# A sorted edge's record in DRAM: 64 bytes at multiples of 64 in place of 24 bytes side by side, in a four-layer graph network kernel

## The chip, the cores and the metric

The kernel runs on one core of one Trainium2 chip. The time is the device time of one execution, in microseconds. Nine executions of the kernel before took 2677.39 to 2699.86 us, with a median of 2693.03 us.

The names of the engines in the profile: PE is TensorE's matrix multiplication and PEld its weight load, DVE is VectorE, ACT is ScalarE, POOL is GpSimd, SP is SyncE, and SPq is SP's queue of DMAs. Transfers issued by SP run one after another on that queue, shared out over 16 DMA engines.

## The reference

The kernel computes four residual graph layers over 3125 nodes with 96 features and 100000 edges that are sorted by destination. Each layer takes the row-wise normalised and rectified features and adds its result to `x`.

```python
h = jnp.maximum(_layernorm(x, axis=-1), 0.0)
x = x + _L0_gnn_ref(h, edge_index)       # 10 hops: out = spmm(out) * 0.9 + h * 0.1
h = jnp.maximum(_layernorm(x, axis=-1), 0.0)
x = x + _L1_gnn_ref(h, src, dst, W, b)   # softmax over each node's incoming edges
h = jnp.maximum(_layernorm(x, axis=-1), 0.0)
x = x + _L2_gnn_ref(h, edge_index, edge_attr, ...)
h = jnp.maximum(_layernorm(x, axis=-1), 0.0)
x = x + _L3_gnn_ref(h, edge_index, ...)  # two graph convolutions
```

What matters for this case is layer 2, the only one that needs data per edge. For every edge it forms a message from the features of both ends and from four edge attributes, and sums the messages of each destination:

```python
node_feat = _mlp(x, W_node, b_node, g_node, beta_node)
edge_feat = _mlp(edge_attr, W_edge, b_edge, g_edge, beta_edge)
row, col = (edge_index[0], edge_index[1])
message = jnp.concatenate([x[row], x[col], edge_feat], axis=1)
message = _mlp(message, W_msg, b_msg, g_msg, beta_msg)
agg = jax.ops.segment_sum(message, col, num_segments=N)
return agg + node_feat
```

`_mlp` is a matrix product, a rectification and a normalisation over all rows (with the mean and the variance over all edges, for the messages).

## The kernel before, in words

All the work is in `narrow` (a second version, `wide`, runs only when a flag says that a bound did not hold; here it doesn't run). Its stages follow one another: a prelude that builds count tables from the edge list, layer 0 with its ten hops, layer 1, layer 2, layer 3. Nodes are kept in `NB` = 25 blocks of 128. A hop is a product of a table of edge counts (`A8`, 25 by 25 blocks of 128 x 128, 8-bit floats) with the features: for each block of nodes 25 weight loads and 25 matmuls (`gather`, L409). What follows a pair of blocks is in `onward`: VectorE scales and adds (L635, L637) and splits the sum into a high and a low half for the next hop.

**Sorting edges.** Layer 2 wants 48128 of the edges grouped by their source, in bins of 125 nodes. These edges are dealt with in three groups `GA` of 125, 125 and 126 columns of 128 edges. `in_bins(g, ...)` works out each edge's place `addr` on VectorE in many small steps and then sends each edge's record to that place. A record is 12 numbers of 16 bits, 24 bytes: the four attributes as high parts, their four low parts, a one, two small numbers that say where the edge's two ends lie, and one unused. The records of 14 columns are put together on POOL in one of two tiles `rec2` (L550 to L553), and then POOL issues one indirect DMA for each column (L555): 128 records, one from each partition, to the rows of `recs[g]` in DRAM that `addr` names. A place is partition-major: `addr` is the partition times `CG` = 152, plus 25 times the bin, plus a rank. So `recs[g]` has 128 x 152 = 19456 places, more than there are edges. The places that no edge takes must hold a harmless record; the prelude fills all places with it from the tile `blank` (L346 to L351), with one store for each group on SP's queue.

The steps of `in_bins` are a generator that `beside` advances twice in each pair of blocks from the second hop on. So the sort runs beside layer 0's hops: VectorE, TensorE and ScalarE work at the hops and at a first pass over the edge attributes (`eps`, L666 to L669, fed by SP's loads L664), and POOL issues the scatters.

**Reading the records back.** At the start of layer 1, `in_fields(g)` (L785) loads a group's records as 128 rows of 152 records (L788, SP's queue, two buffers `recs2`). VectorE takes the eleventh number of each into `rlA`, in six slices (L791) and copies that into `rf` (L797); ScalarE copies the first ten numbers into `rf`, reordered (L796). Then, four places at a time, TensorE turns a piece of `rf` (L803), ScalarE copies it from PSUM (`fts`, L805), and SP stores it to `fields` in DRAM (L807), from where layer 2 reads it. These are generators as well: layer 1's loop over its 25 blocks advances group 0 from block 2 on, group 1 from block 7 and group 2 from block 16. A scheduler decides the final order of the instructions on each engine: it has moved the parts of `in_fields` that need only the load ahead of the loop's order, to layer 1's beginning.

Layer 1's block is 50 matmuls with their weight loads into one of two PSUM buffers `hop` (L816); then `lo` (ScalarE, L819), `both` (VectorE, L821), `den` and `z` (VectorE), a transpose `zp` (L831) that ScalarE copies into `zT` (L833), a product `op` (L835) that is added to `x` (VectorE, L836); then the normalisation of the new rows, whose `hb` is on ScalarE (L394), and two tables `Pt` and `Qt` of layer 2, stored by SP (L853). Each engine goes through its instructions in order, so an instruction that waits holds up those behind it on that engine.

Layer 2 (from 1741 us) fetches rows of 384 bytes from `Pt` by the sources of the edges, with 408 indirect DMAs on POOL (L1024), from DRAM into SBUF; no records are written there.

Of the kernel before, what the change touches and what calls it, by code (L numbers as in the profile page):

```python
# [11 lines left out]
F16 = mybir.dt.float16  # L12
# [9 lines left out]
P = 128  # L22
# [22 lines left out]
GA = [(0, 125), (16000, 125), (32000, 126)]  # L45
BINS, BN = 25, 125
SL, CAP = 6, 768
CG = 152
UA = len(GA) * CG // 4
AHEAD = 1440  # L50
# [16 lines left out]
def narrow(ctx: ExitStack, tc: tile.TileContext, a: dict, out: bass.AP, flag: bass.AP):  # L67


    nc = tc.nc  # L70
    V, S, G, T = nc.vector, nc.scalar, nc.gpsimd, nc.tensor

    const = ctx.enter_context(tc.tile_pool(name="const", bufs=1))
    dram = ctx.enter_context(tc.tile_pool(name="dram", bufs=1, space=DRAM))
# [2 lines left out]
    Pt = dram.tile([NP, 2 * D], F16, name="Pt")  # L77
    Qt = dram.tile([NP + 2 * P, 2 * D], F16, name="Qt")
    Sd = [dram.tile([NP + 2 * P, D], F32, name=f"Sd{i}") for i in range(2)]
    recs = [dram.tile([P * CG, 12], F16, name=f"recs{i}") for i in range(len(GA))]  # L80

    fields = dram.tile([UA, 44, P], F16, name="fields")
    rlT_d = dram.tile([P, Q * 8], F16, name="rlT_d")
# [73 lines left out]
    with tc.tile_pool(name="edges", bufs=1) as sp, tc.tile_pool(name="onehot", bufs=3) as hp, tc.tile_pool(name="handed", bufs=2) as hd, \  # L157
# [119 lines left out]
        for n, g in enumerate(order):  # L277
# [13 lines left out]
            for s in ((0, 1) if n == 0 else (upward,)):  # L291
                line = up if s else down
                at = line.index(g) + 1 if s == upward else 0
                if at < len(line):
                    handed[s] = hd.tile([P, NB], F16, name=f"handed{s}")
                    c = column_of(line[at]) + (0 if s else WIN - 1)
# [45 lines left out]
        for t in Sd:  # L342
            nc.sync.dma_start(t.rearrange("(b p) d -> p b d", p=P), zero[:, None, :D].to_broadcast([P, NB + 2, D]))
        nc.sync.dma_start(Qt[NP:].rearrange("(b p) d -> p b d", p=P),
                          zero.bitcast(F16)[:, None, :2 * D].to_broadcast([P, 2, 2 * D]))
        blank = sp.tile([P, CG, 12], F16, name="blank")  # L346
        G.memset(blank, 0.0)
        G.memset(blank[:, :, 9:10], 200.0)
        G.memset(blank[:, :, 10:11], 4000.0)
        for t in recs:  # L350
            nc.sync.dma_start(t.rearrange("(p c) k -> p (c k)", p=P), blank.rearrange("p c k -> p (c k)"))  # L351


        src = a["edge_attr_T"].rearrange("k (s c) -> (k s) c", s=25)
# [84 lines left out]
    r, m = norm(0, NB)  # L439
# [24 lines left out]
    def in_bins(g, rp, ep):  # L464
# [4 lines left out]
        si, di, b, t, w, mv = (room[:, 1040 + 126 * i:1040 + 126 * i + C] for i in range(6))  # L469
# [60 lines left out]
        p, lo, hi = mv.bitcast(I32), scan.bitcast(I32), t.bitcast(I32)  # L530
# [14 lines left out]
        ea = a["edge_attr_4"][e0:e0 + n].rearrange("(p c) k -> p c k", p=P)  # L545
        for c0 in range(0, C, 14):
            n = min(14, C - c0)
            r = rec2[(c0 // 14) % 2]
            et = rp.tile([P, 14, 4], F32, name="ea2", bufs=2)[:, :n, :]
            G.dma_start(et, ea[:, c0:c0 + n])  # L550
            G.tensor_copy(r[:, :n, 0:4], et)
            G.tensor_tensor(r[:, :n, 4:8], et, r[:, :n, 0:4], ALU.subtract)
            G.tensor_copy(r[:, :n, 9:11], lane2[:, c0:c0 + n, :])  # L553
            for c in range(n):
                ins = G.indirect_dma_start(  # L555
                    out=recs[g], out_offset=bass.IndirectOffsetOnAxis(ap=addr[:, c0 + c:c0 + c + 1], axis=0),
                    in_=r[:, c, :], in_offset=None, bounds_check=P * CG - 1, oob_is_err=False)
                if c0 + c:
                    tc.declare_no_dep(ins.ins, group=f"recs{g}", reason="each edge has a row of its own")
                tc.add_to_no_dep_group(f"recs{g}", ins.ins)  # L560
            yield

    with tc.tile_pool(name="l0", bufs=1) as lp, tc.tile_pool(name="l0p", bufs=3, space=PSUM) as pp:
        A8 = lp.tile([P, NB, NP], F8, name="A8")
        dc = lp.tile([P, NB], F32, name="dc")
        u = up.tile([P, NB, 2 * D + 2], F16, name="u")
        V.memset(u[:, :, 2 * D:], 1.0)
        with tc.tile_pool(name="l0t", bufs=4, space=PSUM) as tp:
            V.memset(none.bitcast(I32), 0)
            for k in range(NB):  # L570
# [12 lines left out]
                if k % 5 == 4:  # L583
                    g = slice(k - 4, k + 1)
                    V.tensor_reduce(cnt_dst[:, g], sums[:, g, :], AX.X, ALU.add)
                    t = small.tile([P, 5], F32, name="deg")
# [16 lines left out]
        em = None  # L603
        tri16 = room[:, 2304:2368].bitcast(F16)
        V.tensor_scalar(tri16, lane, part, None, ALU.is_gt)
        rec2 = [lp.tile([P, 14, 12], F16, name=f"rec2{i}") for i in range(2)]
        for t in rec2:
            G.memset(t, 0.0)
            G.memset(t[:, :, 8:9], 1.0)
        with tc.tile_pool(name="l0e", bufs=3, space=PSUM) as ep, tc.tile_pool(name="l0r", bufs=1) as rp, \  # L610
                tc.tile_pool(name="l0o", bufs=1, space=PSUM) as op:
            binning = itertools.chain(*(in_bins(g, rp, op) for g in range(len(GA))))
            for step in range(K_HOPS):
                last = step == K_HOPS - 1
                whole = up.tile([P, NB, 2 * D + 2], F16, name="u")
# [79 lines left out]
                spare, u = u, new  # L695
# [69 lines left out]
    with tc.tile_pool(name="l1", bufs=1) as lp, tc.tile_pool(name="l1w", bufs=3) as wp, \  # L765
# [19 lines left out]
        def in_fields(g):  # L785

            r = lp.tile([P, CG, 12], F16, name="recs2", bufs=2)
            nc.sync.dma_start(r.rearrange("p c k -> p (c k)"), recs[g].rearrange("(p c) k -> p (c k)", p=P))  # L788
            for i in range(SL):
                c = slice(i * BINS, (i + 1) * BINS if i < SL - 1 else CG)  # L790
                V.tensor_scalar(rlA[:, g * CG + c.start:g * CG + c.stop], r[:, c, 10], relB[:, g * SL + i:g * SL + i + 1], None,  # L791
                                ALU.subtract)
            rf_ = lp.tile([P, CG * 11 + P - 44], F16, name="rf", bufs=2)
            V.memset(rf_[:, CG * 11:], 0.0)
            rf = rf_[:, :CG * 11].rearrange("p (u f j) -> p u f j", f=11, j=4)
            S.activation(rf[:, :, :10, :], r.rearrange("p (u j) f -> p u f j", j=4)[:, :, :10, :], AF.Copy)  # L796
            V.tensor_copy(rf[:, :, 10, :], rlA[:, g * CG:(g + 1) * CG].rearrange("p (u j) -> p u j", j=4))  # L797
            yield
            for u0 in range(0, CG // 4, 4):
                n = min(4, CG // 4 - u0)  # L800
                ps = qp.tile([P, 4, P], F32, name="ft")[:, :n, :]
                for i in range(n):
                    T.matmul(ps[:, i, :], rf_[:, 44 * (u0 + i):44 * (u0 + i) + P], ident16, start=True, stop=True)  # L803
                t = wp.tile([44, 4, P], F16, name="fts")[:, :n, :]
                S.activation(t, ps[:44], AF.Copy)  # L805
                at = g * CG // 4 + u0
                nc.sync.dma_start(fields[at:at + n].rearrange("u f e -> f u e"), t)  # L807
                yield
# [3 lines left out]
        for b in range(NB):  # L812
# [7 lines left out]
            t = wp.tile([P, 2, D], F32, name="both")  # L820
# [17 lines left out]
            r, m = norm(b, 1)  # L838
# [343 lines left out]
    with tc.tile_pool(name="l3", bufs=1) as lp, tc.tile_pool(name="l3w", bufs=3) as wp, \  # L1182
# [78 lines left out]
        for b0 in range(0, NB, 5):  # L1261
            g = slice(b0, b0 + 5)
# [597 lines left out]
```

## Time and profile before

The profile is of one execution that took 2685.9 us; the span from its first to its last instruction is 2683.6 us. Busy time by stage, in us (the windows' bounds are read from the timeline, and rounded):

| window, us | stage | PE | DVE | ACT | POOL | TensorE clock | DMA share |
|---|---|---|---|---|---|---|---|
| 0 to 104 | prelude, first part | 16.27 | 57.10 | 8.08 | 33.35 | 0.93 | 0.27 |
| 104 to 480 | prelude, count tables | 277.92 | 324.27 | 281.25 | 12.30 | 0.93 | 0.04 |
| 480 to 1565 | layer 0, sort of edges | 653.38 | 436.80 | 278.14 | 398.59 | 0.76 | 0.04 |
| 1565 to 1741 | layer 1 | 150.55 | 129.54 | 73.25 | 2.27 | 0.94 | 0.16 |
| 1741 to 2510 | layer 2 | 604.85 | 439.32 | 232.36 | 420.11 | 0.92 | 0.41 |
| 2510 to 2683 | layer 3 | 139.45 | 94.63 | 46.74 | 5.97 | 0.88 | 0.10 |
| whole span | | 1842.4 | 1481.7 | 919.8 | 872.6 | | |

A share over the whole span is a mean over stages with different limits; the table is read a stage at a time. The clock is the share of its full rate that TensorE was granted. The scatters of L555 run from 586.7 to 1254 us, in three bursts, one for each group.

How the profile's lines are read. A group's line has the line of the program, the engine, the operation, out<-in with the tiles' names, the shapes, how often it came, then its busy time in us and the mean of one in ns, and after the second bar the time that the engine stood idle just before these instructions and what ended most of that. A line of the timeline has the start and the duration in us, then engine, line and operation, the count where several were joined, and in brackets the idle time ahead of it with what ended it. "issue" is time in which the engine waited for nothing that the profile shows; "remote" is a wait that the profile puts down to no instruction of this core. A line of windows has the stretch and its length in us, then for PE, PEld, DVE, ACT and POOL the busy time with the count, the clock, the share of the DMA engines and GB/s.

### The profile page before, as it was taken

What the parts mean: (1) busy time and instruction counts of PE and PEld (TensorE: products, weight loads), DVE (VectorE), ACT (ScalarE), POOL (GpSimd) and SP (SyncE); (2) the same over time, 40 slices, a digit from 0 to 9 for tenths busy, and PEclk for the clock granted to TensorE, in tenths of its full rate; (3) what the DMA queues carried; (4) which work ended last, traced back from release to release, by engine and by line L of the source; (5) the groups of instructions that cost most, each with busy time, mean ns of one, the idle gap of its engine ahead of it and who ended that gap; (6) DMA issues with size and microseconds to landing.
All of it is one profiled execution on the core that took longest, in us unless ns stands there. A gap on an engine that the chain in (4) does not pass through costs nothing. (4 is left out here: it accounts for less than half of the span.)

```text
span 2683.6 us, 51385 instructions
## 1 busy us (share of the span) xinstructions
PE 1842.4 (69%) x19447; PEld 1477.7 (55%) x19447; DVE 1481.7 (55%) x4400; ACT 919.8 (34%) x2334; POOL 872.6 (33%) x928
## 2 busy tenths in 40 slices
PE   0477777881366128313999988858888787788698
PEld 0223335760155007202999978646666666677588
DVE  3778999880046006201664587736665555555853
ACT  0488847370166003000331253313333332222340
POOL 4100000017723771675000000065555555554000
PEclk9789999985578558655999999979999999989799
DMA  4100000000000000000000011134444444334200
GB/s 119 57 9 1 1 1 3 8 10 4 4 9 9 4 4 10 5 4 5 10 10 19 2 47 30 32 97 101 107 107 109 106 101 107 89 96 100 55 1 20
DMA packets 133737, 108.21 MB, mean 40 GB/s; under 512 B 93607, under 2 KB 103341, under 8 KB 133479
## 3 DMA queue, kind: packets, MB, share of 16 engines
q1 hardware_dynamic: 106117, 79.60, 11.3%
q0 software_dynamic: 25952, 22.03, 4.5%
q8 instruction: 154, 2.52, 0.4%
q10 hardware_dynamic: 1410, 3.20, 0.4%
q14 instruction: 104, 0.85, 0.1%
HBM read 86.43 MB, written 18.29 MB: 39 GB/s over the span
## 5 line engine op out<-in xcount | busy, mean ns | idle before, releaser
L409 PE MATMUL hop<-u,A 128*128 128x192 f16 (+1 forms) x6250 | 619.6, 253 | 392.2 <-issue 387.4
L409 PEld LDWEIGHTS <-A 128*128 128x128 fp8e4 x6250 | 542.8, 99 | 481.1 <-issue 459.4
L1024 POOL DMA_INDIRECT h<-Pt,srow x408 | 420.1, 1030 | 481.0 <-PE pre L1082 206.5
L635 DVE SCALAR_TENSOR_TENSOR wt<-hop,sc,h 128x96 f32<-128x96 f32 x225 | 69.8, 310 | 569.5 <-remote 434.5
L555 POOL DMA_INDIRECT recs<-rec,x x250 | 245.3, 981 | 262.2 <-DVE wt L637 180.8
L668 ACT ACTIVATE eps<-eps 96x512 f32<-96x512 f32 x196 | 107.0, 569 | 585.0 <-remote 455.8
L1085 DVE SCALAR_TENSOR_TENSOR u<-pre,u 128x384 f16<-128x384 f32 x216 | 119.6, 554 | 311.0 <-ACT u L1084 237.6
L1084 ACT ACTIVATE u<-pre 128x384 f16<-128x384 f32 x216 | 105.9, 490 | 494.8 <-remote 189.1
L286 PE MATMUL cps<-hk,hl 128*128 128x500 f16 x784 | 230.4, 414 | 60.6 <-DVE hl L244 40.0
L1082 PE MATMUL pre<-W3h,eh 96*128 96x96 f16 x1728 | 228.3, 213 | 21.8 <-issue 21.5
L244 DVE TENSOR_TENSOR hk<-ki,keyT 128x4000 f16<-128x4000 f16 x98 | 219.6, 2241 | 34.7 <-PE cps L286 29.6
L1100 PE MATMUL gram<-u 128*97 128x194 f16 x864 | 197.1, 257 | 23.9 <-issue 22.8
L290 ACT ACTIVATE C<-cps 128x500 f32 x269 | 162.7, 605 | 98.1 <-PE cps L289 66.4
L1082 PE MATMUL pre<-W3h,el 96*128 96x96 f16 x864 | 183.1, 212 | 13.6 <-issue 13.2
L286 PEld LDWEIGHTS <-hl 128*128 128x128 f16 x784 | 73.5, 119 | 168.3 <-DVE hl L244 80.3
L555 POOL DMA_INDIRECT recs<-rec,addr x126 | 123.5, 980 | 106.3 <-DVE x L685 64.6
L1082 PEld LDWEIGHTS <-eh 96*128 96x128 f16 x1728 | 137.9, 102 | 26.1 <-issue 25.6
L1065 DVE SCALAR_TENSOR_TENSOR el<-ef,eh 96x512 f16<-96x512 f32 x216 | 147.4, 683 | 7.7 <-issue 7.3
L1100 PEld LDWEIGHTS <-u 128*97 128x97 f16 x864 | 114.2, 132 | 61.5 <-issue 49.5
L669 DVE BATCH_NORM_STATS2 x<-eps 96x6 f32<-96x512 f32 x196 | 134.5, 686 | 22.1 <-issue 11.1
L1064 ACT ACTIVATE eh<-ef 96x512 f16<-96x512 f32 x216 | 126.8, 587 | 22.5 <-PE ef L1062 13.3
L1082 PE MATMUL pre<-qa,ohS 128*128 128x96 f16 x912 | 122.2, 211 | 14.1 <-issue 13.6
(427 smaller groups left out, 3729.1 us busy)
## 6 DMA issues: line engine op xcount, KB each, us to landing
spread<-fields SPq DMA_DIRECT2D x114, 256.0 KB
spread<-rl_d SPq DMA_DIRECT2D x51, 256.0 KB
h<-Pt,srow POOLq DMA_INDIRECT x408
recs<-rec,x POOLq DMA_INDIRECT x250
et<-fields SPq DMA_DIRECT2D x228, 9.0 KB
x<-ea_d SPq DMA_DIRECT2D x195, 18.0 KB
qg<-Qt SPq DMA_DIRECT2D x204, 12.0 KB
Sd<-zero SPq DMA_DIRECT2D x2, 1296.0 KB
```

Of the source, the lines that this page charges most:

```text
L244: V.tensor_tensor(t, pat[:, None, :, :].to_broadcast([P, s, n, c]), val[:, q, :].rearrange("p (s c) -> p s c", s=s)[:, :, None, :].to_broa ...
L286: T.matmul(ps, hl[:, j // 4, :, j % 4], hk[:, j // 2, :, j % 2], start=j == js[0], stop=n == 0 and j == js[-1])
L290: S.activation(C8[:, :, bass.ds(column_of(g), WIN)], ps, AF.Copy)
L409: T.matmul(ps[:, i, :], table[:, k, c0 + (b0 + i) * P:c0 + (b0 + i + 1) * P], u[:, k, :], start=k == 0, stop=k == NB - 1)
L555: ins = G.indirect_dma_start(out=recs[g], out_offset=bass.IndirectOffsetOnAxis(ap=addr[:, c0 + c:c0 + c + 1], axis=0), in_=r[:, c, :], in_ ...
L669: V.bn_stats(stats[:, i % 49, :], ps)
L1024: G.indirect_dma_start(out=pgs[i % len(pgs)][:, c, :], out_offset=None, in_=Pt, in_offset=bass.IndirectOffsetOnAxis(ap=srow[:, k:k + 1], a ...
L1064: S.activation(eh, ps[:D, :], AF.Relu)
L1065: V.scalar_tensor_tensor(el, ps[:D, :], 0.0, eh, ALU.max, ALU.subtract)
L1082: T.matmul(ps[:, c, :], t, w, start=j == 0, stop=j == len(by) - 1)
L1085: V.scalar_tensor_tensor(mm[:, :, D + 2:], ps, 0.0, mm[:, :, :D], ALU.max, ALU.subtract)
L1100: T.matmul(gram, mm[:, c, :D + 1], mm[:, c, :], start=n == 0 and c == 0, stop=n == L - 1 and c == HC - 1)
```

## The change

A record's place in DRAM becomes `RW` = 32 numbers of 16 bits, 64 bytes, and starts at a multiple of 64. Only its first 24 bytes mean anything.

- The fill in the prelude: `blank` holds 8 places, not 152, and the store of each group writes it 19 times for each partition, in pieces of 512 bytes. All 64 bytes of each place are written. Each group's store is 1.25 MB instead of 0.47 MB.
- The scatter: each record's source is 32 numbers from the same start in SBUF. Records in `rec2` still lie 12 apart, so the 20 numbers behind a record are those of the next ones; the tile `rec2_` is 20 numbers longer, so that the last record has something behind it, and is cleared whole.
- The load in layer 1: 24 bytes out of each 64 are read, into the same SBUF tile as before. It is a transfer of 128 x 152 pieces, not of 128 rows.

The counts of instructions do not change, and neither does anything that computes. The scheduler's order in layer 1's first blocks does: on VectorE the first L791 stands nine instructions later than before, behind the second block's first normalisation steps; on ScalarE the first L796 stands behind `zT`, `hb` and the copy into `Wpq`, the second right behind the next `lo`; on SP the third load L788 stands directly behind the three small loads that follow the first two, where before two more stood between; on PE only the order around those blocks moves.

```diff
--- before.py
+++ after.py
@@ -45,6 +45,7 @@
 GA = [(0, 125), (16000, 125), (32000, 126)]
 BINS, BN = 25, 125
 SL, CAP = 6, 768
+RW = 32
 CG = 152
 UA = len(GA) * CG // 4
 AHEAD = 1440
@@ -77,7 +78,7 @@
     Pt = dram.tile([NP, 2 * D], F16, name="Pt")
     Qt = dram.tile([NP + 2 * P, 2 * D], F16, name="Qt")
     Sd = [dram.tile([NP + 2 * P, D], F32, name=f"Sd{i}") for i in range(2)]
-    recs = [dram.tile([P * CG, 12], F16, name=f"recs{i}") for i in range(len(GA))]
+    recs = [dram.tile([P * CG, RW], F16, name=f"recs{i}") for i in range(len(GA))]
 
     fields = dram.tile([UA, 44, P], F16, name="fields")
     rlT_d = dram.tile([P, Q * 8], F16, name="rlT_d")
@@ -343,12 +344,13 @@
             nc.sync.dma_start(t.rearrange("(b p) d -> p b d", p=P), zero[:, None, :D].to_broadcast([P, NB + 2, D]))
         nc.sync.dma_start(Qt[NP:].rearrange("(b p) d -> p b d", p=P),
                           zero.bitcast(F16)[:, None, :2 * D].to_broadcast([P, 2, 2 * D]))
-        blank = sp.tile([P, CG, 12], F16, name="blank")
+        blank = sp.tile([P, 8, RW], F16, name="blank")
         G.memset(blank, 0.0)
         G.memset(blank[:, :, 9:10], 200.0)
         G.memset(blank[:, :, 10:11], 4000.0)
         for t in recs:
-            nc.sync.dma_start(t.rearrange("(p c) k -> p (c k)", p=P), blank.rearrange("p c k -> p (c k)"))
+            nc.sync.dma_start(t.rearrange("(p u c) k -> p u (c k)", p=P, c=8),
+                              blank.rearrange("p c k -> p (c k)")[:, None, :].to_broadcast([P, CG // 8, 8 * RW]))
 
 
         src = a["edge_attr_T"].rearrange("k (s c) -> (k s) c", s=25)
@@ -545,7 +547,7 @@
         ea = a["edge_attr_4"][e0:e0 + n].rearrange("(p c) k -> p c k", p=P)
         for c0 in range(0, C, 14):
             n = min(14, C - c0)
-            r = rec2[(c0 // 14) % 2]
+            r, whole = rec2[(c0 // 14) % 2], rec2_[(c0 // 14) % 2]
             et = rp.tile([P, 14, 4], F32, name="ea2", bufs=2)[:, :n, :]
             G.dma_start(et, ea[:, c0:c0 + n])
             G.tensor_copy(r[:, :n, 0:4], et)
@@ -554,7 +556,7 @@
             for c in range(n):
                 ins = G.indirect_dma_start(
                     out=recs[g], out_offset=bass.IndirectOffsetOnAxis(ap=addr[:, c0 + c:c0 + c + 1], axis=0),
-                    in_=r[:, c, :], in_offset=None, bounds_check=P * CG - 1, oob_is_err=False)
+                    in_=whole[:, 12 * c:12 * c + RW], in_offset=None, bounds_check=P * CG - 1, oob_is_err=False)
                 if c0 + c:
                     tc.declare_no_dep(ins.ins, group=f"recs{g}", reason="each edge has a row of its own")
                 tc.add_to_no_dep_group(f"recs{g}", ins.ins)
@@ -603,9 +605,10 @@
         em = None
         tri16 = room[:, 2304:2368].bitcast(F16)
         V.tensor_scalar(tri16, lane, part, None, ALU.is_gt)
-        rec2 = [lp.tile([P, 14, 12], F16, name=f"rec2{i}") for i in range(2)]
-        for t in rec2:
-            G.memset(t, 0.0)
+        rec2_ = [lp.tile([P, 14 * 12 + RW - 12], F16, name=f"rec2{i}") for i in range(2)]
+        rec2 = [t[:, :14 * 12].rearrange("p (c k) -> p c k", k=12) for t in rec2_]
+        for i, t in enumerate(rec2):
+            G.memset(rec2_[i], 0.0)
             G.memset(t[:, :, 8:9], 1.0)
         with tc.tile_pool(name="l0e", bufs=3, space=PSUM) as ep, tc.tile_pool(name="l0r", bufs=1) as rp, \
                 tc.tile_pool(name="l0o", bufs=1, space=PSUM) as op:
@@ -785,7 +788,7 @@
         def in_fields(g):
 
             r = lp.tile([P, CG, 12], F16, name="recs2", bufs=2)
-            nc.sync.dma_start(r.rearrange("p c k -> p (c k)"), recs[g].rearrange("(p c) k -> p (c k)", p=P))
+            nc.sync.dma_start(r, recs[g].rearrange("(p c) k -> p c k", p=P)[:, :, :12])
             for i in range(SL):
                 c = slice(i * BINS, (i + 1) * BINS if i < SL - 1 else CG)
                 V.tensor_scalar(rlA[:, g * CG + c.start:g * CG + c.stop], r[:, c, 10], relB[:, g * SL + i:g * SL + i + 1], None,
```

## The prediction

> **What bounds the kernel now.** I first read the page's 40-slice strip. TensorE, VectorE and ScalarE together fall almost to nothing three times between a fifth and a half of the span, and POOL is busy exactly there. The costliest groups name the two sides of this:
>
> ```profile
> L635 DVE SCALAR_TENSOR_TENSOR wt<-hop,sc,h 128x96 f32<-128x96 f32 x225 | 69.8, 310 | 569.5 <-remote 434.5
> L555 POOL DMA_INDIRECT recs<-rec,x x250 | 245.3, 981 | 262.2 <-DVE wt L637 180.8
> L1024 POOL DMA_INDIRECT h<-Pt,srow x408 | 420.1, 1030 | 481.0 <-PE pre L1082 206.5
> ```
>
> L555 is the indirect scatter of the sorted edges' records (125, 125 and 126 of them, 128 rows each). Windows cut at the three bursts, with a stretch after them for comparison, and one in layer 2 (us, then busy time and count of PE, PEld, DVE, ACT, POOL; granted clock; DMA share; GB/s):
>
> ```profile
> 587.00:758.00 171.00, 42.33 (x199) 19.99 (x197) 21.08 (x79) 25.41 (x56) 129.12 (x151) 0.54 0.04 5
> 841.00:1012.00 171.00, 36.60 (x163) 16.20 (x162) 13.99 (x60) 9.09 (x21) 129.68 (x152) 0.53 0.04 4
> 1082.00:1254.00 172.00, 38.16 (x176) 15.80 (x174) 7.84 (x24) 4.33 (x12) 130.21 (x152) 0.53 0.04 4
> 1254.00:1565.00 311.00, 302.25 (x3489) 293.44 (x3490) 185.07 (x684) 85.36 (x246) 0.59 (x1) 0.98 0.04 10
> 1758.00:1776.00 18.00, 2.79 (x18) 1.61 (x18) 0.82 (x2) 0.00 (x0) 10.49 (x12) 0.50 0.32 79
> ```
>
> In the bursts PE issues about one matmul per us (538 in 514 us); afterwards 3489 in 311 us. The DMA engines are 4% busy, so bytes are not the limit. The timeline inside a burst shows the rhythm:
>
> ```profile
> 893.92 0.10 PEld L409 LDWEIGHTS <-A 128*128 128x128 fp8e4 x1 [2.70 <-issue]
> 894.59 0.98 POOL L555 DMA_INDIRECT recs<-rec,x  x1 [0.30 <-issue]
> 895.32 0.32 PE L409 MATMUL hop<-u,A 128*128 128x192 f16 x1 [2.48 <-issue]
> 896.72 0.10 PEld L409 LDWEIGHTS <-A 128*128 128x128 fp8e4 x1 [2.70 <-issue]
> ```
>
> One PE instruction, load or matmul, starts each 1.40 us; a scatter takes 0.98 + 0.30 = 1.28 us, and 376 of them 481 us. While they run, layer 0 hardly moves. So a change to the scatter could matter for hundreds of us, if it changed this. The fifth window says that it does not depend on the record: there POOL issues L1024, gathers from DRAM into SBUF with rows of 384 B, back to back, and PE shows the same step:
>
> ```profile
> 1765.58 0.24 PE L1082 MATMUL pre<-W3h,eh 96*128 96x96 f16 x1 [2.56 <-issue]
> 1768.41 0.24 PE L1082 MATMUL pre<-W3h,eh 96*128 96x96 f16 x1 [2.59 <-issue]
> 1771.21 0.24 PE L1082 MATMUL pre<-W3h,el 96*128 96x96 f16 x1 [2.56 <-issue]
> ```
>
> A matmul every 2.8 us with one weight load between is 1.40 us an instruction. Another direction, 16 times the row, the same crawl: it follows POOL's back-to-back indirect DMAs.
>
> The other place touched is the start of layer 1, where the records come back (all from the timeline):
>
> ```profile
> 1574.07 0.79 SPq L788 DMA_DIRECT2D recs<-recs  x2
> 1579.70 0.25 DVE L791 TENSOR_SCALAR rlA<-recs,relB 128x25 f16<-128x25 f16 x1
> 1580.10 2.82 ACT L796 ACTIVATE rf<-recs 128x1520 f16<-128x1520 f16 x1
> 1583.58 2.83 ACT L796 ACTIVATE rf<-recs 128x1520 f16<-128x1520 f16 x1
> 1588.35 0.24 DVE L791 TENSOR_SCALAR rlA<-recs,relB 128x25 f16<-128x25 f16 x1
> ```
>
> The last row is the third group's first use. In the 50 us from 1600 PE is busy 45.1, so layer 1 runs at PE's pace and a late start is not won back.
>
> **The change, part by part.** *Scatter (L555).* Same count, same 128 rows, 64 B in place of 24. The groups' means bound it: 981 ns for 24 B, 1030 ns for 384 B. By bytes in a straight line 40/360 of the 49 ns is 5 ns, times 376 is +2 us, which I take; the ends are +18 us (all 49 ns) and −6 us (every scatter at the shortest seen, 966 ns). The extra 40 bytes run into the neighbouring record of the same tile; no instruction is added.
>
> *Blank fill (L351).* Three stores of 128 rows of 3648 B become three of 2432 pieces of 512 B. In the window 40–48 us the hardware queue moved 3738 packets, mostly the 384-B zero rows, in 77.1% of 16 engines: 98.7 us of engine time, 26.4 ns each. 7296 pieces then hold the engines 7296 × 26.4 / 16 = 12.0 us; before, 1.40 MB at the 400 GB/s of that stretch took 3.5. I cost this at nothing: SP's two loads that VectorE waits for (L335, L178) are issued at 55.50 and 55.94, ahead of L351 at 56.77; behind L351 on SP's queue stand only the edge-attribute stores (L363, L367), then nothing until 100.90; the first scatter over the blanks is at 586.7. Without that cover it would be +8.5 us. The smaller memsets on POOL are off the path.
>
> *Layer 1's load (L788).* Each of the three loads turns from 128 rows of 3648 B into 128 × 152 = 19456 pieces of 24 B, 1216 for each of 16 engines. The trace holds no such read. Nearest rows, as engine time per piece, from three windows' queue lines (packets, MB, share of 16 engines; windows 900–1000, 48–56 and 2511–2522 us):
>
> ```profile
> q0 software_dynamic: 2419, 0.36, 3.6%
> ...
> q10 hardware_dynamic: 32, 0.00, 0.2%
> ...
> q1 hardware_dynamic: 6541, 2.45, 98.5%
> ```
>
> First, the scatters: 0.036 × 16 × 100 us = 57.6 us over the 71 × 128 = 9088 rows issued there, 6.3 ns a 24-B row, several to a packet. Second, a 1.4-KB transfer of tiny packets: 0.002 × 16 × 8 us / 32 = 8.0 ns (6 to 10 by the rounding). Third, 384-B reads: 173.4 us / 6541 = 26.5 ns. So one load takes T = 7.7, 9.7 or 32.2 us. Generation of descriptors is no tighter: the third line alone is 0.6 a ns. A 24-B piece as a packet of its own is nearest to the second row: T = 9.7.
>
> All three loads run one after another on SP's queue. Traffic starts about 1.2 us after the issue (a store issued at 56.28 first shows at about 57.4), so at 1575.3; the groups land at 1575.3 + T, + 2T, + 3T = 1585.0, 1594.7 and 1604.5. The third use stood at 1588.35: +16.1 us. The chain is: ScalarE's second L796 would stand until 1594.7 (1583.58 before), and queued behind it in ScalarE's order are the copies `fts` (L805), `hb` (L394) and `zT` (L833); VectorE's L791 stands in front of the next blocks' sums (L821, L826); PE has two `hop` buffers, one 5-us block of cover, and then waits for those. The new order puts some of the next blocks' work ahead of the first L791, which costs nothing while that work is ready. On SP, the third load now stands ahead of the first `fields`, `Pt` and `Qt` stores, so these wait too; their readers are in layer 2 (`h` waits for `Qt` 174 us after POOL's own work), behind layer 1's last block.
>
> Sum: 0 + 2 + 16 = +18 us. Against the profiled run that is 2683.6 + 2.3 around it + 18 = 2704; the runs' median, 2693.0, lies 7.1 above that run, so I forecast 2711. Own range: 6 to 10 ns gives 3T = 21.9 to 36.5, +9 to +23, and with the scatter's −6 to +18 some 2697 to 2734.
>
> The Trainium skill ("DMA: Bandwidth & Descriptors", section Measured) gives about 10.5 ns a packet for 64 small ones; as an estimate T would be 12.8 us and the sum +27 instead of +18. Its section Specifications says that a transfer under 512 B is a read-modify-write, by which 64 B gains nothing over 24; "Collectives: The Full Stack" (Buffer alignment) holds that 32-byte alignment avoids one, which would favour this change. No run here shows either.
>
> **Rivals.** *A, the load is hidden.* If pieces cost only the bytes they span, 1.25 MB at the 351 GB/s seen at 1576–1578 is 3.5 us: landings at 1578.8, 1582.4, 1585.9, each at or before its use. For it: the scatter rows do share packets. Against: those rows, even packed, are 6.3 ns, and this would be 2.9. Time: 2693 to 2701. Chance 0.18.
>
> *B, pieces cost like 384-B rows.* Cost per piece and not per byte, 12 to 26.5 ns: 3T = 44 to 97, +30 to +83 with no cover, 2723 to 2776. For it: the only well-measured short reads from DRAM are these. Against: 26.5 ns for 384 B is already near the rate of long rows. Chance 0.22.
>
> *C, faster.* The crawl at L555 is a matter of partial or shared 64-byte lines in DRAM, and whole lines lift it. If PE ran the bursts at its later pace, their 538 matmuls would need 48 us of 514: −466, about 2230. It decides from the point where PE's step falls under 1.28 us, the scatter's own. Against it stands the 384-B gather's identical 1.40 us; for it, only that three quarters of layer 0's lost time is in these lines. A lesser form, scatters shorter by a few hundredths of a us, is worth 11 us at 0.03. Chance 0.13 together.
>
> **Numbers.** The forecast has 0.47, the rest as above. This kernel's runs tell about 0.3%, 8 us, from no change. Faster by more: C, 0.13. Within: A and the forecast's lowest edge, 0.20. Slower: 0.67. The range leaves out C and the top third of B (0.07): 2688 to 2757.
>
> **What would show it.** Right: L555 near 0.98 us with PE's 1.40-us step beside it; the bursts' three windows within 2 us of 171; the first L791 at about 6 us, the third group's at about 30 us after the L788 issue; layer 1's end later by the same amount, layers 2 and 3 unchanged in length. Wrong: a burst with PE at full pace (C), L791 at its old distance (A), or landings 15 to 30 us apart (B). Also wrong would be a VectorE wait for a load at 57–75 us, which I costed at nothing.

## The result, and the profile after

The changed kernel takes 2715.57 us (median of 10 runs, 2712.10 to 2724.36) and the kernel before 2692.52 us (31 runs, 2677.39 to 2706.16): the ratio is 1.009, with a 95% interval of 1.0072 to 1.0108. The medians lie 23 us apart, where 18 were forecast. Its profiled run has a span of 2709.3 us, 25.7 us more than the 2683.6 before. Lines have moved by two or three: L555 is now L557, L788 is L791, L791 is L794, L796 is L799, L1024 is L1027.

Where the 25.7 us are follows from the first starts of a few rows in both profiles:

| from the profile's rows, us | before | after | difference |
|---|---|---|---|
| first scatter starts | 586.7 | 587.6 | +0.9 |
| last scatter starts | 1253.6 | 1256.9 | +3.3 |
| first load of records is issued | 1574.07 | 1577.82 | +3.75 |
| first gather of layer 2 starts | 1742.1 | 1771.9 | +29.8 |
| first load `sd` of layer 3's node sums | 2511.0 | 2538.5 | +27.5 |
| end of the span | 2683.6 | 2709.3 | +25.7 |

Layer 1 alone accounts for the sum: +26.0 from its first load to layer 2's first gather. The +3.75 ahead of it and the -4 behind it are of the size in which runs of one kernel differ (e2_pieces below, which has no 64-byte places, also comes to its first load late, at 1577.42).

**The scatter bursts are as they were.** Windows of the changed kernel over the second burst, over the stretch behind the third, and over the gathers of layer 2 (columns as before):

```profile
844.00:1015.00 171.00, 36.76 (x164) 15.28 (x162) 14.08 (x61) 9.09 (x22) 129.54 (x152) 0.53 0.06 8
1258.00:1568.00 310.00, 303.41 (x3490) 293.93 (x3491) 184.42 (x681) 84.69 (x242) 0.00 (x0) 0.98 0.04 10
1788.00:1806.00 18.00, 2.50 (x15) 1.48 (x16) 0.14 (x1) 0.00 (x0) 10.38 (x11) 0.50 0.30 77
```

171 us, 164 matmuls and 152 POOL instructions in the burst, against 171, 163 and 152 before. The bytes doubled (8 GB/s for 4), and the scatters' packets, as many as before, took more of the DMA engines' time (queue q0 in 900 to 1000 us: 2427 packets at 5.4%, before 2419 at 3.6%). Nothing came of it in the burst. The timeline in the burst:

```profile
893.46 0.32 PE L411 MATMUL hop<-u,A 128*128 128x192 f16 x1 [2.48 <-issue]
893.73 0.98 POOL L557 DMA_INDIRECT recs<-rec,x  x1 [0.30 <-issue]
894.86 0.10 PEld L411 LDWEIGHTS <-A 128*128 128x128 fp8e4 x1 [2.69 <-issue]
896.26 0.32 PE L411 MATMUL hop<-u,A 128*128 128x192 f16 x1 [2.48 <-issue]
```

Still one PE instruction each 1.40 us, still 0.98 + 0.30 us a scatter, now with 64 whole bytes a record.

**Layer 1 waits for its records.** The timeline of SP and VectorE at its start:

```profile
1577.82 13.39 SPq L791 DMA_DIRECT2D recs<-recs  x2
1591.26 12.44 SPq L114 DMA_DIRECT2D W_g<-in_L_gnn_W  x2
1592.56 0.24 DVE L794 TENSOR_SCALAR rlA<-recs,relB 128x25 f16<-128x25 f16 x1 [6.17 <-DMA recs<-recs]
1604.33 0.53 SPq L791 DMA_DIRECT2D recs<-recs  x1
1605.33 0.24 DVE L794 TENSOR_SCALAR rlA<-recs,relB 128x25 f16<-128x25 f16 x1 [7.48 <-DMA recs<-recs]
1620.10 0.24 DVE L794 TENSOR_SCALAR rlA<-recs,relB 128x25 f16<-128x25 f16 x1 [6.55 <-DMA recs<-recs]
```

The three groups are usable 14.7, 27.5 and 42.3 us after the first issue; before, their first uses stood at 5.6, 8.2 and 14.3 us and waited for nothing. The second stands 12.77 us behind the first: that is one load, 12.77 us / 1216 = 10.5 ns for each piece on an engine. Note what SP shows: it is held for 12.44 us while it issues two small weight loads, and most of the 13.39 us in the row above is the second load's own issue, held behind the first. In the kernel before, the two weight loads took 0.90 us:

```profile
1574.91 0.90 SPq L113 DMA_DIRECT2D W_g<-in_L_gnn_W  x2
```

Each hold ends some 1.5 us before the load ahead is used, so I read it as SP waiting until that load has drained. The third load is issued only after that, and with this gap its interval is 14.77 us. The waits in 1578 to 1622 us (us in total, times, the longest):

```profile
DVE rlA L794 <- DMA recs<-recs: 20.2, 3, 7.5
ACT rf L799 <- DMA recs<-recs: 16.8, 2, 9.7
PE ft L806 <- ACT fts L808: 12.9, 2, 9.5
PE ft L806 <- ACT rf L799: 7.3, 1, 7.3
```

VectorE and ScalarE wait for the records, and PE in its own order for what they would have made.

### The profile page after: what moved, and what is told of

It reads as the page before. It is cut to its first block, busy times and chain, and to the rows that moved or that the text cites. A ratio compares the mean times of both kernels' runs of the same rounds, so it can differ in the third digit from the quotient of the medians.

```text
span 2709.3 us, 51386 instructions
## 1 busy us (share of the span) xinstructions
PE 1846.7 (68%) x19447; PEld 1480.3 (55%) x19447; DVE 1482.4 (55%) x4400; ACT 921.6 (34%) x2334; POOL 867.8 (32%) x928
## 4 chain that ended last, share of the span: by engine, by line
PE 43%; issue 21%; DVE 11%; ACT 5%; SPq 2%; DMA 1%; another core or an unknown queue 1%; POOL 0%; ACTq 0%; POOLq 0%; DVEq 0%
PE hop L411 19%; PE pre L1085 10%; PE gram L1103 3%; PE ef L1065 2%; PE segA L1135 2%; PE segs L1114 2%; ACT A L581 1%; PE eps L669 1%; ACT x L694 1%; DVE x L672 1%; PE btp L577 1%; ACT hb L396 1%; PE hop L819 1%; SPq L114 1%
## 5 line engine op out<-in xcount | busy, mean ns | idle before, releaser
L1027 POOL DMA_INDIRECT h<-Pt,srow x408 | 417.9, 1024 | 511.8 <-PE pre L1085 208.5
L557 POOL DMA_INDIRECT recs<-rec,x x250 | 245.2, 981 | 265.9 <-DVE wt L640 183.8
L557 POOL DMA_INDIRECT recs<-rec,addr x126 | 123.4, 979 | 106.2 <-DVE x L688 64.8
L672 DVE BATCH_NORM_STATS2 x<-eps 96x6 f32<-96x512 f32 x196 | 134.5, 686 | 22.2 <-ACT eps L671 14.7
L400 ACT ACTIVATE u<-wt 128x96 f16<-128x96 f32 x225 | 62.5, 278 | 219.7 <-DVE wt L640 216.8
```

The lines of the kernel that those rows point to most:

```text
L557: ins = G.indirect_dma_start(out=recs[g], out_offset=bass.IndirectOffsetOnAxis(ap=addr[:, c0 + c:c0 + c + 1], axis=0), in_=whole[:, 12 * c ...
L672: V.bn_stats(stats[:, i % 49, :], ps)
L1027: G.indirect_dma_start(out=pgs[i % len(pgs)][:, c, :], out_offset=None, in_=Pt, in_offset=bass.IndirectOffsetOnAxis(ap=srow[:, k:k + 1], a ...
```

## The experiments

e5_halves, e6_actq, e9_actpack and e10_gate ran on another Trainium2 chip than the rest. There the kernel before takes 2026.1 us, not 2693; more of this below. Each ratio is to runs of the kernel before in the same session, on the same chip, and loss in us is the difference of the two medians. Where e1_whole, e2_pieces, e3_early and e4_48 were run, the kernel before took 2705.46 us, some 13 more than the 2693 on which their expectations in us rest; they are read by the difference.

**Layer 1 reads whole places.** Scatter and fill stay as in the change:

```diff
-            r = lp.tile([P, CG, 12], F16, name="recs2", bufs=2)
-            nc.sync.dma_start(r, recs[g].rearrange("(p c) k -> p c k", p=P)[:, :, :12])
+            r = lp.tile([P, CG, RW], F16, name="recs2", bufs=2)
+            nc.sync.dma_start(r.rearrange("p c k -> p (c k)"), recs[g].rearrange("(p c) k -> p (c k)", p=P))
```

> Records, fill and scatter stay at 64 bytes; layer 1 reads a group's places whole, 128 rows of 9728 bytes, into a larger tile. Theory (the added time is the number of pieces in layer 1's loads and nothing else): 1.25 MB at the 351 GB/s seen before is about 3.5 us a load, the first L791 about 6 to 8 us after the first load's issue, the third group's about 20 us; time within 4 us of before, some 2690 to 2697 us. Rival (64-byte scatters and the larger fill carry part of it; the changed kernel reached layer 1 3.7 us later): 2697 us or more, with layer 1's first load issued 3 to 4 us later than before.

2703.68 us against 2705.46: ratio 0.9989 (0.9977 to 1.0001). ScalarE's first L799 starts 7.6 us after the first issue, VectorE's first L794 9.4 us after it (6 to 8 were expected) and the third group's 17.4. 64-byte places, their scatter and their larger fill cost nothing that can be measured, and bring nothing; the whole loss is the load in pieces. (The first load was issued at 1580.5 here, later than in the changed kernel, with no loss to show for it, so the shift ahead of layer 1 is not a cost of the 64-byte places.)

**Pieces without the 64-byte places.** The kernel before, with a load that leaves out the unused number of each record:

```diff
-            nc.sync.dma_start(r.rearrange("p c k -> p (c k)"), recs[g].rearrange("(p c) k -> p (c k)", p=P))
+            nc.sync.dma_start(r[:, :, :11], recs[g].rearrange("(p c) k -> p c k", p=P)[:, :, :11])
```

> The kernel before with one part of the change alone: records stay 24 bytes side by side, but the load takes only 22 of each 24 bytes, so it is 19456 pieces a group again. Theory (each piece has a price, whatever its place): some 12.7 us a load, 10.4 ns for each of an engine's 1216 pieces, groups usable at about 14.7, 27.5 and 42 us after the first issue as in the changed kernel, and 2710 to 2720 us. Rival one (the 64-byte places cost part of it): 2697 to 2710 us. Rival two (the price hangs on the stride in DRAM, a piece of 64 bytes each being another line): loads well under 12 us, at the bytes' share (24 of 64) about 5 us, and 2693 to 2700 us.

2735.10 against 2705.46 us, ratio 1.0126 (1.0103 to 1.0148): 30 us lost, somewhat more than the changed kernel loses. VectorE's first uses in it:

```profile
1596.44 0.25 DVE L791 TENSOR_SCALAR rlA<-recs,relB 128x25 f16<-128x25 f16 x1 [10.53 <-DMA recs<-recs]
1611.13 0.24 DVE L791 TENSOR_SCALAR rlA<-recs,relB 128x25 f16<-128x25 f16 x1 [9.39 <-DMA recs<-recs]
1628.97 0.25 DVE L791 TENSOR_SCALAR rlA<-recs,relB 128x25 f16<-128x25 f16 x1 [10.11 <-DMA recs<-recs]
```

14.69 us from the first to the second, 12.1 ns a piece. The price does not need the 64-byte stride: the same number of pieces, lying almost side by side, is dearer still. Both rivals fall; the theory's size (12.7 us a load) was too small for these pieces.

**48 bytes of each 64.**

```diff
-            nc.sync.dma_start(r, recs[g].rearrange("(p c) k -> p c k", p=P)[:, :, :12])
+            nc.sync.dma_start(r, recs[g].rearrange("(p c) k -> p c k", p=P)[:, :, :24])
```

> The changed kernel, but layer 1 reads 48 bytes of each 64, into a tile with 48 bytes a record; the same 19456 pieces. Theory (price per piece): 12.5 to 13.5 us a load, 2712 to 2720 us as the changed kernel. Rival (price by bytes): 25 us a load, third group usable near 80 us after the first issue, about 2750 us.

2729.64 against 2705.46 us, ratio 1.0080 (1.0056 to 1.0105), as the changed kernel's. Groups two and three are usable at 1606.75 and 1619.13, after 1592.54 for the first: 14.2 and 12.4 us (11.7 and 10.2 ns a piece), not 25. Twice the bytes cost about the same; the price is per piece.

**Twice the pieces.**

```diff
-            nc.sync.dma_start(r, recs[g].rearrange("(p c) k -> p c k", p=P)[:, :, :12])
+            for k in (0, 6):
+                nc.sync.dma_start(r[:, :, k:k + 6], recs[g].rearrange("(p c) k -> p c k", p=P)[:, :, k:k + 6])
```

> The changed kernel with each layer-1 load split in two: the first and the last 12 bytes of each 64-byte place, so 38912 pieces a group and the same bytes in all. Theory (a price per piece, 10 ns of an engine): some 25 us a group, the groups usable near 27, 52 and 78 us after the first issue (14.7, 27.5 and 42 in the changed kernel); 35 us on top of its 23, ratio 1.019 to 1.025. Rival (a price by bytes): as the changed kernel, 1.007 to 1.011.

2084.06 against 2026.10 us, ratio 1.0284 (1.0251 to 1.0317): 58 us lost, at the theory's side and a little beyond it.

```profile
1143.01 0.24 DVE L795 TENSOR_SCALAR rlA<-recs,relB 128x25 f16<-128x25 f16 x1 [17.99 <-DMA recs<-recs]
1166.40 0.24 DVE L795 TENSOR_SCALAR rlA<-recs,relB 128x25 f16<-128x25 f16 x1 [18.04 <-DMA recs<-recs]
1191.57 0.24 DVE L795 TENSOR_SCALAR rlA<-recs,relB 128x25 f16<-128x25 f16 x1 [16.86 <-DMA recs<-recs]
```

23.39 us from group to group, 9.6 ns for each of 2432 pieces of 12 bytes. So 12, 24 and 48 bytes all cost about 10 ns (9.6 to 11.7); the 22-byte pieces, at 12.1, are the dearest seen.

**A second queue.** The second group's load is issued on ScalarE's queue:

```diff
-            nc.sync.dma_start(r, recs[g].rearrange("(p c) k -> p c k", p=P)[:, :, :12])
+            (nc.scalar if g == 1 else nc.sync).dma_start(r, recs[g].rearrange("(p c) k -> p c k", p=P)[:, :, :12])
```

> The changed kernel with the second group's load issued from ScalarE's DMA queue, the others from SP's. Theory A (the pieces are paid in the 16 DMA engines that both queues share): the first two groups run side by side and are both usable only near 27 us after the issue; no gain, ratio 1.008 to 1.014. Theory B (each queue makes its descriptors at 10 ns a piece and engine, and two queues go side by side): both usable near 15 us, the third near 28; ratio 1.003 to 1.006.

2051.82 against 2026.10 us, ratio 1.0130 (1.0099 to 1.0160). SP's load is issued at 1117.66 and ScalarE's at 1117.77; VectorE and ScalarE get both at once:

```profile
1144.63 0.24 DVE L794 TENSOR_SCALAR rlA<-recs,relB 128x25 f16<-128x25 f16 x1 [18.51 <-DMA recs<-recs]
1144.62 5.55 ACT L799 ACTIVATE rf<-recs 128x1520 f16<-128x1520 f16 x2 [19.81 <-DMA recs<-recs]
```

27 us after the issue: two queues side by side take as long for two loads as one queue does. The pieces are paid in something that both queues share, and another queue beside the first buys nothing: theory B falls. That it is the 16 DMA engines, as theory A says, is not shown; a shared maker of descriptors would look the same here.

**The pieces read early, from SP.** During layer 0 a copy in DRAM packs the records, and layer 1 loads rows of 3648 bytes:

```diff
+    packed = [dram.tile([P * CG, 12], F16, name=f"packed{i}") for i in range(len(GA))]
...
+                    if slot == 100:
+                        for g in range(len(GA)):
+                            nc.sync.dma_start(packed[g].rearrange("(p c) k -> p c k", p=P),
+                                              recs[g].rearrange("(p c) k -> p c k", p=P)[:, :, :12])
...
-            nc.sync.dma_start(r, recs[g].rearrange("(p c) k -> p c k", p=P)[:, :, :12])
+            nc.sync.dma_start(r.rearrange("p c k -> p (c k)"), packed[g].rearrange("(p c) k -> p (c k)", p=P))
```

> The changed kernel with the pieces read early: in hop 7 of layer 0, when all scatters are done, SP copies each group's 24 used bytes from the 64-byte places into a packed array in DRAM, and layer 1 loads that as 128 rows of 3648 bytes. Theory: the same 3 x 12.7 us of pieces are paid where nothing waits for them, layer 1 starts as before, 2690 to 2698 us. Rival (the pieces cost the same wherever they are, by blocking SP's queue or the DMA engines under the hops): 2705 us or more.

2809.28 against 2705.46 us, ratio 1.0401 (1.0374 to 1.0427): 104 us lost, and the theory is wrong. The scheduler put the copies not together into hop 7 but each some 50 us behind its own group's last scatter, at 811.5, 1107.0 and 1379.5 us, in the middle of SP's loads of edge attributes. The last of them, on SP and PE:

```profile
1379.47 0.49 SPq L688 DMA_DIRECT2D packed<-recs  x1
1383.41 40.05 SPq L668 DMA_DIRECT2D x<-ea_d  x4
...
1383.43 4.34 PE L412 MATMUL hop<-u,A 128*128 128x192 f16 x50
1422.12 1.04 PE L670 MATMUL eps<-x,We 128*128 128x512 f16 x2 [34.35 <-DMA x<-ea_d]
```

SP's next loads are held until the copy has drained, PE comes to a matmul over those attributes and stands for 34 us. Three such stalls, of 37.5, 35.3 and 34.4 us, are the 104 us. From DRAM to DRAM the pieces also take about three times as long (SP is held for 40.05 us behind one copy, and for 12.44 behind one load in the changed kernel). One half of the theory held: with whole rows to load, layer 1 takes 160.5 us from the first to the last of its matmuls on `h`, as in the kernel before (160.6).

**The same copy on ScalarE's queue.**

```diff
-                            nc.sync.dma_start(packed[g].rearrange("(p c) k -> p c k", p=P),
+                            nc.scalar.dma_start(packed[g].rearrange("(p c) k -> p c k", p=P),
```

> The early packing again (the 24 used bytes of each place copied to a packed array in DRAM during layer 0), with the copies on ScalarE's DMA queue, where nothing is queued behind them. Theory (e3_early lost 104 us because the edge-attribute loads of the first pass stood behind the copies on SP's queue, some 36 us for each of three): ratio 0.998 to 1.003. Rival (the copies slow the hops wherever they are issued, by the shared DMA engines): 1.01 or more.

2366.11 against 2026.10 us, ratio 1.168 (1.1653 to 1.1706). It tells nothing of its question, for a reason that lies outside it. The waits of ScalarE, the two lines on the scatters:

```profile
ACT u L401 <- DMA recs<-rec,x: 200.1, 2, 104.3
ACT u L401 <- DMA recs<-rec,addr: 90.0, 1, 90.0
```

On this chip the hops run ahead of the scatters, so ScalarE reaches the copy some 100 us before its group's scatters are done, waits for them in its order, and the hops with it: 290 us of waits, where 340 were lost. What an early read costs where nothing stands behind it was not settled.

**The uses held back.** L791 and L796 are made to depend on the block at which layer 1's loop calls for them (`now[0]`); `rel` stands for `relB` in L791, and `none_` is a tile of zeros:

```diff
+            gate = lp.tile([P, 1], F32, name="gate", bufs=3)
+            V.tensor_scalar(gate, x[:, now[0], 0:1], 0.0, 1.0, ALU.mult, ALU.add)
+            rel = lp.tile([P, SL], F32, name="rel", bufs=3)
+            V.tensor_scalar(rel, relB[:, g * SL:(g + 1) * SL], gate, None, ALU.mult)
...
-            S.activation(rf[:, :, :10, :], r.rearrange("p (u j) f -> p u f j", j=4)[:, :, :10, :], AF.Copy)
+            S.activation(rf[:, :, :10, :], r.rearrange("p (u j) f -> p u f j", j=4)[:, :, :10, :], AF.Identity, scale=gate, bias=none_)
```

> The changed kernel with the use of the loaded records held back to its place in layer 1's loop: L791's and L796's operands are made to depend on block 2's, 7's and 16's row of x (times zero), so that the second and the third group's first uses can't stand ahead of the blocks in VectorE's and ScalarE's order. The loads are the same. Theory (the time was lost by in-order waits on VectorE and ScalarE ahead of ready work): only the first group's wait is left, some 5 us; ratio 1.000 to 1.004. Rival (it was lost on SP's queue, where the stores of fields, Pt and Qt stand behind the loads, or in the DMA engines): 1.007 or more.

2040.35 against 2026.10 us, ratio 1.0070 (1.0047 to 1.0093): 14 us lost, outside the theory's range and at the rival's lower edge. So it was run again beside the changed kernel, on one chip:

> The changed kernel once more, beside the next two. The layer-1 part of its 23 us does not hang on layer 0's pace, so it should again lose 20 to 28 us to the kernel before, whether this chip runs that in about 2700 us (ratio 1.008 to 1.010) or in about 2030 us as in the last four runs (1.010 to 1.014). Rival (its loss came from the slow bursts of layer 0): no loss where PE is not slowed by them.

> The kernel with the gated uses once more, on the same chip as the changed kernel. Theory (the changed kernel's loss has two parts, in-order waits of VectorE and ScalarE in front of ready work, about 10 us, and SP's queue, where small loads and the first fields, Pt and Qt stores stand behind the pieces, about 14 us): 12 to 16 us slower than before, 8 to 12 us faster than the changed kernel. Rival (one cause only): either 0 to 4 us or 20 and more slower than before.

The changed kernel: 2716.16 against 2686.95 us, ratio 1.0115 (1.0089 to 1.0141), 29 us, just above what was expected. The gated one: 2710.83 us, ratio 1.0086 (1.0063 to 1.0108), 24 us. Gating won only 5 us of the 29. Its waits in 1575 to 1622 us show why:

```profile
PE ft L809 <- ACT fts L811: 19.7, 1, 19.7
ACT fts L811 <- DMA fields<-fts: 19.5, 1, 19.5
```

No wait for records is left, and a single one has taken its place. SP's stores of `fields` stand behind the second and third load's pieces; three buffers `fts` fill up, ScalarE can't take another, and PE stops for 19.7 us. On SP:

```profile
1604.90 0.53 SPq L791 DMA_DIRECT2D recs<-recs  x1
1605.53 11.52 SPq L813 DMA_DIRECT2D fields<-fts  x1
```

The 24 us lie where the rival had them (20 and more), and my split into 10 and 14 us is wrong. But "one cause" doesn't describe it either: before the gating the engines waited for the records themselves, after it for the buffers behind the records' load. Both waits lie over the same time, and taking off one alone shows the other.

**The later loads off SP's queue too.** The gated kernel, with the second and third load on ScalarE's queue at blocks 3 and 11:

```diff
+            if g:
+                V.tensor_scalar(r[:, 0, :1], x[:, now[0], 0:1], 0.0, None, ALU.mult)
-            nc.sync.dma_start(r, recs[g].rearrange("(p c) k -> p c k", p=P)[:, :, :12])
+            (nc.scalar if g else nc.sync).dma_start(r, recs[g].rearrange("(p c) k -> p c k", p=P)[:, :, :12])
+            if g:
+                yield
...
+            if b in (3, 11):
+                next(turning[b // 8 + 1])
```

> The gated uses, and besides the second and the third group's loads leave SP's queue: they are issued on ScalarE's DMA queue, at blocks 3 and 11, some blocks ahead of their use. Only the first group's pieces are left ahead of anything. Theory: 3 to 8 us slower than before. Rival (the pieces slow layer 1's stores and loads through the shared 16 DMA engines, whatever the queue): 12 us or more slower than before.

2690.61 against 2686.95 us, ratio 1.0007 (0.9987 to 1.0026). Layer 1's matmuls on `h` in the kernel before, the changed, the gated and this one (count, ns shortest/median/longest, start of the first and the last):

```profile
L816 PE MATMUL hop<-h,C x625: 243/246/368, 1566.8 to 1727.4; 128*128 128x192 f16 x157
L819 PE MATMUL hop<-h,C x625: 243/246/368, 1570.6 to 1757.0; 128*128 128x192 f16 x157
L825 PE MATMUL hop<-h,C x625: 243/246/368, 1567.3 to 1746.7; 128*128 128x192 f16 x157
L829 PE MATMUL hop<-h,C x625: 243/246/368, 1572.5 to 1734.3; 128*128 128x192 f16 x157
```

That is 160.6, 186.4 (186.8 in a_again), 179.4 and 161.8 us. On the other chip the gated kernel took 179.0 us for them, and e9_actpack, which loads whole rows, 160.7. So the gated loss in layer 1 is 18 to 19 us on both chips; the 14 and 24 us of the medians differ by what lies outside layer 1. In this run the same three loads of 19456 pieces are made, and the loss is gone. Moving the loads without the gating was tried only for one of them, in e6_actq, which still lost 26 us.

**Half the scatters.** In the kernel before, to price the bursts:

```diff
-            for c in range(n):
+            for c in range(0, n, 2):
...
-        V.tensor_scalar(flag, off[:, 1:2], -1.0, 1.0, ALU.mult, ALU.add)
+        V.tensor_scalar(flag, off[:, 1:2], 0.0, 0.0, ALU.mult, ALU.add)
```

> The kernel before with every second scatter of records left out (188 of 376; half of the records stay blank, so layer 2's sums are not the reference's, and the flag for the second version is held at zero). It prices the bursts. If PE runs at one instruction per 1.40 us during them, as in the profile of before, half of them gone saves about half of the 466 us that I put on them, 200 to 250 us. On a chip like that of the last four runs, where PE keeps its pace, only the wait of layer 1 for the last scatter can go, up to 30 us.

2398.92 against 2686.95 us, ratio 0.893 (0.8901 to 0.8959): 288 us, more than expected. The edit leaves 189 scatters (63 in each group), so 187 are left out, not 188, and each is worth 1.54 us, above its own 1.28. Most of the difference can be read from the bursts. The second one, columns as before:

```profile
751.00:840.20 89.20, 46.59 (x275) 28.86 (x274) 19.72 (x78) 12.24 (x29) 70.40 (x91) 0.65 0.05 7
```

The three bursts take 267 us, 250 less than the 517 of the kernel before, counted from the first scatter to the end of the last. And PE gets through 801 matmuls in them, against 542 before: 259 more, some 23 us at the pace of 3489 in 311 us. Together that is 273 of the 285 us between the two spans. The second part was not foreseen: the scatters follow each other at the same step as before (0.98 + 0.30 us, in runs of 7 and not 14), yet PE does 3.0 matmuls per us where it did 1.05. So the step of the scatters alone doesn't set PE's pace; what does is open.

**The other chip.** In e6_actq's profile, with the same 64-byte scatters at the same step, a window over the first burst:

```profile
587.00:759.00 172.00, 158.77 (x1752) 147.04 (x1750) 139.25 (x467) 130.38 (x297) 131.09 (x151) 1.00 0.10 18
```

And from PE's timeline in the second:

```profile
894.03 4.34 PE L411 MATMUL hop<-u,A 128*128 128x192 f16 x50
```

1752 matmuls beside 151 POOL instructions, where the first chip has 163 to 199 in a burst; 50 of them in 4.34 us with no gap. In layer 2 it is the same: in the 18 us from 1330, some 16 us behind the first gather, PE does 267 matmuls beside 14 POOL instructions; in the first chip's window from 1788 above, as far behind its first gather, it does 15 beside 11. So the crawl of PE beside POOL's indirect DMAs doesn't follow from the program alone: it came on one of the two chips.

## Why the prediction was right

**Direction, size and place held**: slower, by 23 us for 18 forecast, all of it in layer 1's load.

*Scatter, +2 us.* It is nothing: the mean of L557 is 981 ns for 250 of them, as L555's was, and e1_whole closes the question. The +2 came from a straight line to the 384-byte gather, which has no support at 64 bytes.

*Fill, nothing.* It held. SP spends 8.28 us on the three issues where it spent 2.11, and VectorE uses `fr` at 59.21 us, where it had done so at 59.38.

*The price of a piece, 8.0 ns.* This is the term that was mis-sized: 10.5 ns were measured, T = 12.77 us for 9.7, just past the upper end of 10 that I gave to that row. That it came so near is in part luck. The row's 8.0 ns were the packets' share of the engines' time over their number, from 32 tiny packets at a share printed as 0.2%. By the same working the changed kernel's own pieces come to 16.6 ns (138.7% of 16 engines from 1577 to 1592 us, 20025 packets). A share above 100% means that the times of packets overlap, so the working does not give a price, and 16.6 ns would have pointed to rival B. My check on the making of descriptors fails too: 0.6 a ns in the third row is less than the 2 a ns that T = 9.7 asks for, so it left a slower maker possible. The 12.77 us that were measured are 1.5 a ns.

The Trainium skill's figure ("DMA: Bandwidth & Descriptors", section Measured), about 10.5 ns a packet for loads issued from GpSimd, is what these loads from SP showed. The sum by it, +27 us, is nearer than the text's +18 to the 25.7 between the two spans; from the 23 between the medians the two are about equally far.

*Three loads in a row.* Nearly: the third use came at 42.3 us after the issue. 1.2 + 3 x 12.77 gives 39.5. Of the other 2.8 us 0.8 are the first load's and 2.0 the third's longer interval, behind an issue that came late: I took issues on SP for free, and SP was held 12.44 us in front of it. (The list of signs gave "about 6 us" for the first use; my own landing at 1585.0 meant 10.9, and it was 14.7.)

*Who waits.* The named chain is the one in the waits. That nothing of the delay is covered held as well: the third use moved by 28.0 us, layer 1 by 26.0.

*The stores behind the loads, at nothing.* Here the reasoning failed, hidden by the larger wait (in the changed kernel ScalarE waited 3.8 us for a buffer `fts`): I looked for who reads `fields`, `Pt` and `Qt`, in layer 2, and not for who needs their source buffers back. e10_again shows that this alone stops PE for 19.7 us.

**The rivals.** A fell: the pieces cost their number, not their bytes. B fell just short: 10.5 ns, where it began at 12; the 22-byte pieces of e2_pieces would have been in it. C fell: with whole 64-byte places PE's step is 1.40 us as before. But my reason, that the crawl follows POOL's back-to-back indirect DMAs, was only part of it. On the other chip they run without it, and in e8_half, on the first, PE goes nearly three times as fast beside the same step. What differs between the chips is not shown by any run here.

The skill's two rules on short writes: it calls a transfer under 512 bytes a read-modify-write (section Specifications), from which I took that 64 bytes gain nothing over 24. No run here shows such a read, but the outcome agrees: e1_whole gains nothing, and the scatters' packets took more of the DMA engines' time, not less. (The unchanged 981 ns are POOL's time, not that of the write.) For the gain from alignment that "Collectives: The Full Stack" (Buffer alignment) would promise, e1_whole leaves no room beyond 0.2%.

## What to carry to other kernels

Before a contiguous load is turned into pieces, multiply their number per DMA engine by 10 to 12 ns, which is what pieces of 12 to 48 bytes cost here: 1216 pieces of 24 bytes were 12.8 us a load, where whole rows with 2.7 times the bytes cost nothing that could be measured. A long load on a queue has two faces: engines that wait for its data in order, and stores queued behind it whose buffers don't come free; look for both, because a repair of one alone (5 of 29 us here) shows only the other. A cheaper record doesn't help where the cost lies in issuing its DMA.

## What the runs showed of the hardware that was not expected

- Two Trainium2 chips ran the kernel before in 2687 to 2705 and in 2026 us. By the changed kernel's profile and e6_actq's, the difference lies in the two stages in which POOL issues indirect DMAs: 983 against 520 us from the first scatter to layer 1, 767 against 565 in layer 2. In the first of them PE does one instruction per 1.40 us on one chip and 50 matmuls in 4.34 us on the other.
- On the slower chip, runs of 7 scatters at the same step of 1.28 us left PE 3.0 matmuls per us, runs of 14 left it 1.05 (e8_half).
- SP is held at its next issue while a load of many pieces drains: 12.44 us at two weight loads behind 19456 pieces, 40 us at the loads behind the copy from DRAM to DRAM.
- The share of the DMA engines' time goes above 1 where pieces are short (1.48 in the 10 us from 1590 in the changed kernel): the packets' times overlap, so a short packet's duration times its count is no estimate of a transfer.
